# Where statistics, held results and late loads stand in the order of a routed expert kernel

## The chip, the cores and the metric

The kernel runs on one core of one Trainium2 chip. The metric is the device time of one execution in microseconds. The kernel before has a median of 445.12 us over three runs (444.80 to 446.07). One further execution was taken by the hardware profiler; its own time is 444.96 us, and its span, from the first instruction of the program to the last, is 443.2 us. All times inside the kernel are counted from the start of that span.

## The reference

The input x has 32 sequences of 256 tokens with 128 features: 8192 tokens. Two residual branches are computed, each behind a layer norm that is scaled and shifted per sequence.

```python
mod = (_silu(c) @ wmod).reshape(32, 6, 1, -1)
sa, ca, ga, sb, cb, gb = (mod[:, i] for i in range(6))
ga = (2 * (ga >= 0) - 1) * jnp.maximum(jnp.abs(ga), 0.25)      # gb likewise
h = _layernorm(x) * (1 + ca) + sa
g = sigmoid(h @ Wg.T + bg);  a = sigmoid(h @ Wd.T + bd);  v = h @ Wv.T + bv
x = x + ga * (prefix_scan((1 - a) * v, a) * g)                  # h_t = a_t h_{t-1} + x_t
h = _layernorm(x) * (1 + cb) + sb
logits = h @ gate_w.T + gate_b
vals, idx = top_k(softmax(logits), 2)                           # 2 of 8 experts
y[n, e] = relu(h[n] @ w1[e] + b1[e]) @ w2[e] + b2[e]            # hidden width 512
x = x + gb * sum over the two chosen experts of vals * y
```

The reference computes all eight experts for every token and gives six of them weight zero. The kernel computes the two chosen ones only, by sorting tokens to experts.

## The kernel before, in words

The 8192 tokens are cut into 16 supertiles of 512 tokens (s = 0 to 15). Each supertile passes through four steps, which the text calls by their functions: `a_norm` (statistics and normalisation for the first branch), `a_mix` (the first branch, with the scan), `a_res` (the residual, and the second layer norm) and `a_route` (logits, the choice of two experts, and the place of each of the 1024 token-expert pairs). The steps are written in a staggered order: round t does `a_norm(t)`, `a_mix(t-1)`, `a_res(t-2)` and `a_route(t-3)`; the first rounds follow the string `HEAD`. The routing of supertile s is called Rs below. Its last result that others wait for is `pi` (line 471), the rows to which the pairs go; just before it TensorE counts pairs into `pq` (line 454).

GpSimd then writes the rows of the pairs into a table in DRAM, `reg`, eight indirect DMAs for each supertile (line 499, `reg<-rw,pi`). All pairs of one expert lie together in `reg`. So the second branch works in blocks of 256 rows of one expert (68 blocks always, three more if the routing needs them). Some supertiles end with a small table (`table`) that says which blocks are full by then: 5 blocks after R2, 9 after R3, 13 after R4, then 17, 21, 25, 29 after R8, 37 after R10, 45 after R12, and all after R15.

A block passes through `b_load` (SyncE reads the block's expert and row from the table, loads the rows `xr`, line 584, and the expert's first weights `ww`, line 590), `b_in` (TensorE turns the rows into `pbx`, line 597, ScalarE and VectorE split them into `xs`, lines 599 and 600), `b_up` (twelve matmuls `p`, lines 617 to 619, and the activations `hh`) and `b_down` (sixteen matmuls `pby`, line 635, and the scaled result `yt`, line 639). Two indirect DMAs on GpSimd write a block's results to `yd` in DRAM (line 499 again, `yd<-yt,xi`), one row for each pair. One call of `b_step`, step i, does `b_in` of block i, `b_up` of block i-1 and `b_down` of block i-2, and loads up to four blocks ahead (`LOOK`). Five buffers hold `ww`, so the weights of block n wait for `b_up` of block n-5.

All indirect DMAs stand in one order on GpSimd: the scatters to `reg` and those to `yd` are numbered 1 to 264 in that order below (128 and 136). `drip` puts scatters to `reg` into it, one to three after each step. `results_out` puts scatters to `yd` into it, and leaves the youngest results back while routing is still going on. How many blocks' results stay back is the second argument in line 751:

```python
results_out(K * T, NJ * min(min(i - 1, EASE) + max(i - HOLD0, 0), HOLD) if alive or sending else max(len(results) - NJ, 0))
```

With `EASE` 3, `HOLD0` 24 and `HOLD` 9 that is three blocks up to step 24, then one more with each step, up to nine. A load of `xr` waits for the scatters to `reg` that stand before it when it is written (line 586).

At the end come the sums. A supertile's sum reads its two `yd` halves (`c_load`, line 705, tile `yk`, two DMAs of 256 KB), adds them, scales and adds the residual (`c_add`, lines 714, 696 and 716, tile `ot`, on VectorE), and stores the rows (line 717). `ended` holds the supertiles whose last block is done: block 52 ends supertiles 0 to 9, block 58 ends 10 to 12, block 62 ends 13, block 66 ends 14, and 15 comes after all. Each step loads one sum; the sum that was loaded three steps before (`CLAG`) is added in the same step. A `yk` load waits for all scatters to `yd` that stand before it.

The steps of the supertiles are written with priorities (`AHEAD`), and a list scheduler makes each engine's order from them. Within an engine the order is fixed from then on. One manual order is in it: the statistics of `a_norm` (`stats`, line 307) stay behind `placed[-1]`, the last entry of a list that `a_route` fills with its `pi` for the first three supertiles (line 472).

Of the kernel before, what the change touches and what calls it, by code (L numbers as in the profile page):

```python
# [17 lines left out]
ORDER = mybir.DependencyInfo(mybir.DependencyClass.NoSync, mybir.DependencyReason.DATA)  # L18
# [8 lines left out]
T = 4  # L27
# [6 lines left out]

XE = 3
EARLY = 3
PW = 3

AHEAD = (0, 200, 300, 400)
# [1 line left out]
BACK = 2  # L41
SKIP = 8

FIRST = 6
THREE = 7

ALWAYS = 68
# [4 lines left out]

EASE = 3
HOLD0 = 24
HOLD = 9
XRB = 9
OTB = 6
YTB = 7 + HOLD
CLAG = 3
HALF = 15  # L60

LN1G = {**{s: 1 for s in range(12)}, 12: 2, 14: 2}
# [3 lines left out]
def adaln_moe(ctx: ExitStack, tc: tile.TileContext, x, Wg, bg, Wv, bv, Wd, bd,  # L66
              gate_w, gate_b, w1, b1, w2, b2, c, wmod, out):
    nc = tc.nc
    NB, S, D = x.shape
    E, _, H = w1.shape  # L70
# [12 lines left out]
    of = out.rearrange("b s d -> (b s) d")  # L83
# [9 lines left out]
    def tokens(dram, r, n):  # L93
        return dram[r:r + n].rearrange("(q p j) d -> p q (j d)", p=P, j=JB)

    def tiles(t):
        return t.rearrange("p (q j) d -> p q (j d)", j=JB)
# [9 lines left out]
    xa = cp.tile([P, NS, T, D], F32, name="xa")  # L107
# [134 lines left out]
    def late_constants():  # L242
        b2f = wk.tile([P, T, D], F32, tag="ot", name="b2f", bufs=OTB)
        nc.gpsimd.memset(b2f, 0.0)
        for h in range(4):
            for j in range(T):
                r = (h * T + j) * E
                nc.sync.dma_start(b2f[r:r + E, j], b2)
        nc.vector.tensor_copy(b2x, b2f)
        lower = slice(P // 2, P)  # L250
        nc.vector.tensor_tensor(b2x[lower], b2f[lower], b2x[lower], op=ALU.subtract)


        sT3 = cp.tile([P, 3, NB], F32, name="sT3")
        nc.vector.tensor_copy(sT3, sT.unsqueeze(1).to_broadcast([P, 3, NB]))
        pr = psa.tile([P, 512], F32, tag="pz", bufs=2, name="pr")
        nc.tensor.matmul(pr[:N3, :D], sT3.rearrange("p a b -> p (a b)"), wm[:, 5 * D:], start=True, stop=True)
        mr = cp.tile([N3, D], F32, name="mr")
        guarded(mr, pr[:N3, :D], [N3, D], 1.0, "gr")
        nc.vector.tensor_copy(mr3, mr)  # L260
        for i in (1, 2, 2):
            w = slice(i * NB, (i + 1) * NB)
            nc.vector.tensor_tensor(mr[w], mr[w], mr3[w], op=ALU.subtract)
            nc.vector.tensor_copy(mr3[w], mr[w])

        nc.vector.tensor_tensor(sel, ident[:N3, 0:NB], ident[:N3, NB:2 * NB], op=ALU.add)
        nc.vector.tensor_tensor(sel, sel, ident[:N3, 2 * NB:N3], op=ALU.add)
# [29 lines left out]
    f = nc.sync.dma_start(reg[E * CAP:E * CAP + BLK].rearrange("(p t) d -> p t d", p=P), pad)  # L297
# [5 lines left out]
    def stats(mv, src, name, behind=None):  # L303
        n = src.shape[1]
        st = wk.tile([P, T, 6], F32, tag=f"st{name[0]}", name=f"st{name}")
        for j in range(n):
            w = nc.vector.bn_stats(st[:, j], src[:, j])
            if behind:
                tc.add_manual_dep(w.ins, behind.name, ORDER, reason="not ahead of the first supertiles that route")
        for j in range(n):  # L310
            nc.vector.bn_aggr(mv[:, j], st[:, j])

    def rsqrt(mv, name, s):
# [3 lines left out]
        def t1(nm, dt=F32):  # L317
            return wk.tile([P, n, 1], dt, tag=f"{nm}{name[0]}{n}", name=f"{nm}{name}")

        v, y, r = t1("nv"), t1("ny"), t1("nr")  # L320
        if s < PW:
            nc.vector.tensor_scalar(v, mv[:, :, 1:2], 1e-5, RSQ ** -2, op0=ALU.add, op1=ALU.mult)
# [17 lines left out]
    placed = []  # L340
    ln1 = {}

    def a_norm(s):
        g = LN1G.get(s, 0)
        if g:
            mv = wk.tile([P, g * T, 2], F32, tag=f"mva{g}", name=f"mva{s}")
            for i in range(g):
                stats(mv[:, i * T:(i + 1) * T], xa[:, s + i], f"a{s + i}", placed[-1] if placed else None)
            y, r = rsqrt(mv, f"a{s}", s)
            for i in range(g):  # L350
                ln1[s + i] = (y[:, i * T:(i + 1) * T], r[:, i * T:(i + 1) * T])
        y, r = ln1[s]
        xn = wk.tile([P, T, D], F32, tag="xn", name=f"xn{s}")
        for j in range(T):
            nc.scalar.activation(xn[:, j], xa[:, s, j], AF.Identity, scale=y[:, j], bias=r[:, j])  # L355
        return dict(s=s, xn=xn)

    def early(s, tag, name, bufs=1):

        if s < EARLY:  # L360
            return psb.tile([P, ST], F32, tag=tag, name=name, bufs=bufs)
# [54 lines left out]
    def a_route(a, base):  # L416
        s, xn = a["s"], a["xn"]
# [51 lines left out]
        nc.vector.tensor_reduce(pf, op_, axis=AX.X, op=ALU.add)  # L469
        pi = wk.tile([P, T * K], I32, tag="pi", name=f"pi{s}", bufs=3)  # L470
        w = nc.vector.tensor_copy(pi, pf.rearrange("p t k -> p (t k)"))
        if s < EARLY:
            placed.append(w.ins)
        sm = wk.tile([P, T], F32, tag="sm", name=f"sm{s}")
        nc.vector.tensor_reduce(sm, e8, axis=AX.X, op=ALU.add)
        rc = wk.tile([P, T], F32, tag="rc", name=f"rc{s}")
# [174 lines left out]
    results = []  # L651

    def results_out(most, left=0):

        for _ in range(min(most, len(results) - left)):
            results.pop(0)()

    def c_base(s):
# [21 lines left out]
        nc.tensor.matmul(pz, dgT, b2x.rearrange("p t d -> p (t d)"), start=True, stop=True)  # L680
        t = wk.tile([P, T, D], F32, tag="ot", name=f"tb2{s}", bufs=OTB)
        nc.scalar.activation(t.rearrange("p t d -> p (t d)"), pz, AF.Copy)
# [15 lines left out]
    def c_load(s):  # L698
        yk = wk.tile([P, T, K, RW], F32, tag="rw", name=f"yk{s}", bufs=4)
        yk = yk.rearrange("p t k r -> p (t k r)")[:, :K * T * D].rearrange("p (k t d) -> p k t d", k=K, t=T)  # L700
        step = JB if s >= HALF else T
        for j0 in range(0, T, step):
            for k in range(K):
                r = k * N + s * ST + j0 * P
                w = nc.sync.dma_start(tiles(yk[:, k, j0:j0 + step]), tokens(yd, r, step * P))
                tc.add_to_no_dep_group("yrows", w.ins)
        return s, yk, step

    def c_add(s, yk, step, queue):
        g = spread(s, "pz", 2)  # L710
        ot = wk.tile([P, T, D], F32, tag="ot", name=f"ot{s}", bufs=OTB)
        for j0 in range(0, T, step):
            js = slice(j0, j0 + step)
            nc.vector.tensor_tensor(ot[:, js], yk[:, 0, js], yk[:, 1, js], op=ALU.add)  # L714
            scaled(ot, g, range(j0 // JB, (j0 + step) // JB))
            nc.vector.tensor_tensor(ot[:, js], ot[:, js], xa[:, s, js], op=ALU.add)
            queue.dma_start(tokens(of, s * ST + j0 * P, step * P), tiles(ot[:, js]))


    blocks = []  # L720
    flow = []
    ended = []
    adding = []
    nload = 0
    based = 0
    sums = True
    LOOK = 4

    def b_step():

        nonlocal nload
        nonlocal based
        i = len(flow)
        while nload < len(blocks) and nload < i + 1 + LOOK:
            tb, q, ends = blocks[nload]
            blocks[nload] = b_load(nload, tb, q)
            blocks[nload]["ends"] = ends
            nload += 1
        b = blocks[i] if i < len(blocks) else None
        flow.append(b)  # L740
        if b:
            b_in(b)
        if i >= 1 and flow[i - 1]:
            b_up(flow[i - 1])
            drip(1 if alive else 3)
            if len(results) > NJ and not (alive or sending):
                results_out(1)
        if i >= 2 and flow[i - 2]:
            b_down(flow[i - 2])
            ended.extend(flow[i - 2]["ends"])  # L750
            results_out(K * T, NJ * min(min(i - 1, EASE) + max(i - HOLD0, 0), HOLD) if alive or sending else max(len(results) - NJ, 0))
        if not sums:
            return
        if not (alive or sending) and based < NS:
            c_base(based)
            based += 1
        if len(adding) >= CLAG or (adding and not ended and i >= len(blocks)):
            c_add(*adding.pop(0), nc.sync if i <= len(blocks) else nc.scalar)
        if ended:
            results_out(len(results))  # L760
            adding.append(c_load(ended.pop(0)))

    slot = 0
    alive = True
# [26 lines left out]
    for t, todo in enumerate(steps):  # L791
        def step3(s):
            nonlocal base, done
            with tc.high_priority(AHEAD[3] * (s >= EARLY)):
                base = a_route(st[s], base)
# [22 lines left out]
        def step2(s):  # L818
            with tc.high_priority(AHEAD[2] * (s >= EARLY)):
                a_res(st[s])  # L820

        def step1(s):
            with tc.high_priority(AHEAD[1] * (s >= EARLY)):
                a_mix(st[s])

        def step0(s):
            with tc.high_priority(AHEAD[0] * (s >= EARLY)):
                st[s] = a_norm(s)

        for i, s in todo:  # L830
            (step0, step1, step2, step3)[i](s)
            drip(3 if t < THREE else 2 if len(sending) > K * T else 1)
            if t >= FIRST:
                between()
# [59 lines left out]
```

## Time and profile before

| what | value |
|---|---|
| median of three runs | 445.12 us |
| profiled execution: its time / its span | 444.96 / 443.2 us |
| TensorE busy, matmuls (PE) | 366.6 us, 83% |
| TensorE busy, weight loads (PEld) | 321.5 us, 73% |
| VectorE (DVE) busy | 326.2 us, 74% |
| ScalarE (ACT) busy | 291.5 us, 66% |
| GpSimd (POOL) busy | 285.0 us, 64% |
| scatters to `reg`, `yd` (line 499) | 128 and 136, 986 and 1013 ns each |
| DMA over the span | 89.59 MB, 202 GB/s on average |

The page gives the busy share of each engine in 40 slices, the granted TensorE clock and the DMA rate in the same slices. The list of pieces in order of time gives, for each instruction, its start, its duration, the engine, the line, the tiles, and in brackets how long the engine sat idle before it and what ended that. A GpSimd scatter counts as busy for about 0.97 us, and the next one starts some 0.3 us after it.

### The profile page before, as it was taken

Reading aid. Unit: us, or ns where it says so; the run is one execution under the profiler, and the core shown is the slowest. Engines: PE = TensorE matmul, PEld = TensorE weight load, DVE = VectorE, ACT = ScalarE, POOL = GpSimd, SP = SyncE. Lnnn points to the kernel's source line nnn. Section 1 sums busy time; section 2 is a strip of 40 time slices with the busy share of each in tenths; the row PEclk is TensorE's granted clock in tenths of the full one; section 3 lists DMA queues with packets and bytes.
Section 4 is the critical chain, followed back from the end, with each engine's and each line's share of the span. In section 5 each row is a group of like instructions: output and inputs, shape, how many; then the busy total and the mean of one; then the engine's idle time right before and its main releaser. Section 6 shows DMA issues by size and latency. Waiting matters only on the chain.

```text
span 443.2 us, 11140 instructions
## 1 busy us (share of the span) xinstructions
PE 366.6 (83%) x2713; PEld 321.5 (73%) x2713; DVE 326.2 (74%) x1752; ACT 291.5 (66%) x721; POOL 285.0 (64%) x300
## 2 busy tenths in 40 slices
PE   4766465469999999999999999999389997499950
PEld 3333241328899889889989999999279997499940
DVE  6778889998878989978878877977337630346675
ACT  3765363476988998989778777666236666177630
POOL 4644857070577777777777777777777777555560
PEclk9988566588999999999999999999879999699995
DMA  7998311048438475655553886686189774799996
GB/s 196 370 321 248 137 42 45 4 123 297 150 96 246 124 209 169 182 161 173 172 173 114 260 277 197 185 275 173 50 265 304 219 221 148 233 342 362 352 271 197
DMA packets 54357, 89.59 MB, mean 202 GB/s; under 512 B 8366, under 2 KB 39292, under 8 KB 54294
## 3 DMA queue, kind: packets, MB, share of 16 engines
q1 hardware_dynamic: 44656, 70.87, 53.4%
q0 software_dynamic: 8480, 16.93, 10.8%
q10 hardware_dynamic: 1158, 1.07, 0.7%
q8 instruction: 25, 0.41, 0.4%
q14 instruction: 38, 0.31, 0.2%
HBM read 62.32 MB, written 27.04 MB: 202 GB/s over the span
## 4 chain that ended last, share of the span: by engine, by line
PE 57%; DMA 14%; DVE 11%; issue 6%; ACT 4%; POOL 4%; SPq 3%; POOLq 0%; DVEq 0%; ACTq 0%
PE pby L635 21%; PE pz L377 6%; PE p L617 6%; PE p L618 6%; PE p L619 6%; DMA yk<-yd 4%; DMA yd<-yt,xi 4%; PE pbx L597 3%; PE pl L428 3%; POOL reg L499 2%; DMA reg<-rw,pi 2%; PE pb L431 2%; DMA wr<-in_L_ffn_w_dram 2%; ACT xm L413 1%; POOL yd L499 1%
## 5 line engine op out<-in xcount | busy, mean ns | idle before, releaser
L499 POOL DMA_INDIRECT yd<-yt,xi x136 | 137.8, 1013 | 66.5 <-ACT yt L639 30.0
L499 POOL DMA_INDIRECT reg<-rw,pi x128 | 126.2, 986 | 61.6 <-issue 41.9
L635 PE MATMUL pby<-wr,hh 128*128 x1088 | 150.5, 276 | 0.3 <-ACT hh L625 0.3
L635 PEld LDWEIGHTS pby<-wr,hh 128*128 128x128 f32 x1088 | 137.7, 192 | 9.3 <-issue 6.9
L625 ACT ACTIVATE hh<-p,ww 128x256 f32<-128x256 f32 x219 | 93.1, 474 | 28.6 <-PE p L619 21.8
L617 PE MATMUL p<-xs,ww 128*128 128x256 f32 x272 | 86.2, 317 | 1.2 <-DVE cnt L798 0.3
L618 PE MATMUL p<-xs,ww 128*128 128x256 f32 x272 | 78.2, 288 | 0.0
L619 PE MATMUL p<-xs,ww 128*128 128x256 f32 x272 | 77.9, 287 | 0.0
L377 PE MATMUL pz<-h,wT 128*128 128x512 f32 x96 | 58.6, 728 | 3.7 <-ACT h L372 2.2
L639 ACT ACTIVATE yt<-pby,xr 128x128 f32<-128x128 f32 x136 | 42.7, 367 | 24.3 <-PE pby L635 24.3
L617 PEld LDWEIGHTS p<-xs,ww 128*128 128x128 f32 x272 | 52.5, 193 | 3.5 <-ACT ta L381 1.1
L618 PEld LDWEIGHTS p<-xs,ww 128*128 128x128 f32 x272 | 53.0, 195 | 0.5 <-issue 0.5
L619 PEld LDWEIGHTS p<-xs,ww 128*128 128x128 f32 x272 | 52.6, 193 | 0.2 <-issue 0.2
L597 PE MATMUL pbx<-ident,xr 128*128 128x128 f32 x136 | 27.1, 282 | 21.2 <-DMA xr<-reg 11.9
L600 DVE TENSOR_TENSOR xs<-pbx,xs 128x256 fp32r<-128x256 f32 x68 | 28.3, 416 | 20.4 <-ACT xs L599 20.2
L599 ACT ACTIVATE xs<-pbx 128x256 fp32r<-128x256 f32 x68 | 26.4, 388 | 20.2 <-PE pbx L597 20.1
L413 ACT ACTIVATE xm<-xa,nrb,nyb 128x128 f32<-128x128 f32 x64 | 26.5, 484 | 12.8 <-DVE nrb L336 12.8
L714 DVE TENSOR_TENSOR ot<-yk 128x512 f32<-128x512 f32 (+1 forms) x17 | 11.2, 658 | 31.4 <-DMA yk<-yd 30.8
L597 PEld LDWEIGHTS pbx<-ident,xr 128*128 128x128 f32 x136 | 17.1, 146 | 23.5 <-issue 9.9
L377 PEld LDWEIGHTS pz<-h,wT 128*128 128x128 f32 x96 | 19.4, 232 | 19.7 <-issue 12.9
L355 ACT ACTIVATE xn<-xa,nra,nya 128x128 f32<-128x128 f32 x64 | 26.4, 488 | 6.5 <-DVE nra L336 6.5
L623 DVE TENSOR_SCALAR hh<-p,ww 128x256 f32<-128x256 f32 x53 | 25.2, 476 | 5.0 <-ACT hh L625 4.7
(195 smaller groups left out, 645.8 us busy)
## 6 DMA issues: line engine op xcount, KB each, us to landing
ww<-wd SPq DMA_DIRECT2D x68, 514.0 KB
xr<-reg SPq DMA_DIRECT2D x68, 130.0 KB
yk<-yd SPq DMA_DIRECT2D x30, 256.0 KB
wd<-wh SPq DMA_DIRECT2D x8, 514.0 KB
xa<-in_L_attn_x_dram SPq DMA_DIRECT2D x16, 256.0 KB
out_dram<-ot SPq DMA_DIRECT2D x12, 256.0 KB
yd<-yt,xi POOLq DMA_INDIRECT x136
w1s<-in_L_ffn_w_dram SPq DMA_DIRECT2D x8, 256.0 KB
```

Of the source, the lines that this page charges most:

```text
L355: nc.scalar.activation(xn[:, j], xa[:, s, j], AF.Identity, scale=y[:, j], bias=r[:, j])
L377: nc.tensor.matmul(z, wT[:, i], h1, start=True, stop=True)
L413: nc.scalar.activation(xn[:, j], xt[:, j], AF.Identity, scale=y[:, j], bias=r[:, j])
L499: w = nc.gpsimd.indirect_dma_start(in_offset=None, **args).ins
L597: nc.tensor.transpose(px[:, j * P:(j + 1) * P], xr[:, j, 0:D], ident)
L600: w = nc.vector.tensor_tensor(xs[:, 1], px, xs[:, 0], op=ALU.subtract)
L617: nc.tensor.matmul(z, hi, xs[:, 0], start=True, stop=False)
L618: nc.tensor.matmul(z, hi, xs[:, 1], start=False, stop=False)
L619: nc.tensor.matmul(z, lo, xs[:, 0], start=False, stop=True)
L625: nc.scalar.activation(hh[:, k], p1[:, k - k0], AF.Relu, bias=bias)
L635: nc.tensor.matmul(py[:, j * D:(j + 1) * D], hh[:, k, j * P:(j + 1) * P], we[:, k * D:(k + 1) * D], start=(j == 0 and k == 0), stop=(j == ...
L639: nc.scalar.activation(yt[:, j], py[:, j * D:(j + 1) * D], AF.Copy, scale=xr[:, j, D:D + 1])
```

## The change

Four things change together.

- Statistics: `placed` gets the `pi` of every supertile, and the statistics of `a_norm(s)` stay behind the one of supertile s-5, though never behind one older than the third.
- Blocks: `FIRST` goes from 6 to 5, so that steps of blocks are written from round 5 on.
- Held results: `HOLD` goes from 9 to 14. `YTB`, the number of `yt` buffers, follows from 16 to 21; `OTB`, the number of `ot` buffers, goes from 6 to 5.
- Sums: the first step in which a supertile has ended puts all results into the order and only notes its number (`first`); loads begin `DELAY` = 3 steps later. While more than `MANY` = 5 supertiles are waiting, a step loads (and adds) two sums instead of one.

```diff
-FIRST = 6
+FIRST = 5
...
-HOLD = 9
+HOLD = 14
 XRB = 9
-OTB = 6
+OTB = 5
 YTB = 7 + HOLD
 CLAG = 3
+DELAY = 3
+MANY = 5
...
-                stats(mv[:, i * T:(i + 1) * T], xa[:, s + i], f"a{s + i}", placed[-1] if placed else None)
+                stats(mv[:, i * T:(i + 1) * T], xa[:, s + i], f"a{s + i}", placed[min(len(placed) - 1, max(s - BEHIND, EARLY - 1))] if placed else None)
...
-        if s < EARLY:
-            placed.append(w.ins)
+        placed.append(w.ins)
...
-        if len(adding) >= CLAG or (adding and not ended and i >= len(blocks)):
-            c_add(*adding.pop(0), nc.sync if i <= len(blocks) else nc.scalar)
-        if ended:
+        if ended and first is None:
             results_out(len(results))
-            adding.append(c_load(ended.pop(0)))
+            first = i
+        for _ in range(2 if len(ended) > MANY else 1):
+            if len(adding) >= CLAG or (adding and not ended and i >= len(blocks)):
+                c_add(*adding.pop(0), nc.sync if i <= len(blocks) else nc.scalar)
+            if ended and i >= first + DELAY:
+                results_out(len(results))
+                adding.append(c_load(ended.pop(0)))
```

`BEHIND` is 5. No instruction is added or removed: the same 264 scatters, 136 block loads, sums and matmuls run in another order.

More of the change, by code (lines that the diff above doesn't have):

```diff
@@ L36 @@
 EARLY = 3
+BEHIND = 5
 PW = 3
@@ L308, in stats @@
             if behind:
-                tc.add_manual_dep(w.ins, behind.name, ORDER, reason="not ahead of the first supertiles that route")
+                tc.add_manual_dep(w.ins, behind.name, ORDER, reason="not ahead of earlier supertiles that route")
         for j in range(n):
@@ L725, in adaln_moe @@
     based = 0
+    first = None
     sums = True
@@ L731, in b_step @@
         nonlocal nload
-        nonlocal based
+        nonlocal based, first
         i = len(flow)
```

## The prediction

> **What bounds the kernel now.** I read the slices first, then GpSimd's pieces in order of time, then the waits of SyncE's queue, then the two places where TensorE stands still.
>
> ```profile
> PE   4766465469999999999999999999389997499950
> POOL 4644857070577777777777777777777777555560
> PEclk9988566588999999999999999999879999699995
> 117.35 0.96 POOL L499 DMA_INDIRECT reg<-rw,pi  x1 [3.29 <-DVE stb L307]
> 318.64 0.96 POOL L499 DMA_INDIRECT reg<-rw,pi  x1 [0.30 <-DMA yd<-yt,xi]
> 383.63 1.45 POOL L499 DMA_INDIRECT yd<-yt,xi  x1 [0.30 <-issue]
> 388.63 1.12 POOL L499 DMA_INDIRECT yd<-yt,xi  x1 [3.54 <-ACT yt L639]
> ```
>
> TensorE is full from about 100 us. GpSimd's 7 looks loose, but it is full too: from 117.35 to 383.63 us a scatter follows every 1.30 us without a gap (35th to 240th: 266.3 us over 205). The 318.64 row is the last scatter to `reg`.
>
> ```profile
> SPq L584 <- DMA reg<-rw,pi: 106.6, 31, 18.3
> SPq L705 <- DMA yd<-yt,xi: 13.2, 6, 10.9
> 323.31 0.66 PE L597 MATMUL pbx<-ident,xr 128*128 128x128 f32 x2 [9.47 <-DMA xr<-reg]
> 378.20 0.92 SPq L705 DMA_DIRECT2D yk<-yd  x2
> 381.75 0.69 DVE L714 TENSOR_TENSOR ot<-yk 128x512 f32<-128x512 f32 x1 [13.20 <-DMA yk<-yd]
> 382.36 0.42 DVE L600 TENSOR_TENSOR xs<-pbx,xs 128x256 fp32r<-128x256 f32 x1
> 372.80:386.80 14.00, 5.10 (x35) 4.84 (x34) 2.96 (x9) 2.69 (x7) 9.54 (x10) 0.76 0.60 182
> 386.80:426.20 39.40, 38.96 (x345) 38.26 (x343) 24.91 (x59) 27.14 (x73) 21.71 (x21) 1.00 1.01 339
> ```
>
> Both standstills are GpSimd's lateness. Block 45 needs the last scatter to `reg` (318.64, landed 2.3 us later) and starts at 323.31, 9.5 us late. The first sum's load waits for the 234th scatter until 378.20; its add (381.75) stands before block 57's `xs` (382.36) on VectorE, so TensorE loses 8.9 us of the 14 from 372.8. From 386.8 the DMAs are full (share 1.01 at 339 GB/s; the last columns of the window rows are clock, share, rate). So GpSimd's place in its order, and then DMA bytes, set the end.
>
> **Part 1, statistics and earlier blocks.** In the built order, statistics of supertiles 8 to 11 leave the stretch between R2's `pi` and R3's logits: 16 of line 307 at 0.22 us, 16 of line 311 at 0.09, four rows of twelve small ones at 0.15, 9 to 12 us of VectorE work. Only supertile 8's four (0.9 us) stood before R3's last norm; the rest filled waits. In exchange block 0's rows come before R3's logits on TensorE: they need R2's last scatter (76.0 + 2.3), so `xr` issues at 78.5 and lands at 80.6; before, R3's logits began at 80.70. That cancels the 0.9 us. The moved work, 10 us, lands between 100 and 297 us, where VectorE is busy 166 of 197 us: nothing, while that slack lasts.
>
> The blocks are the real move. Blocks 0 to 5 now stand before R4's count. Between the counts of R3 and R4 the order has 78 up-matmuls at 0.13 us, 50 pairs of down-matmuls at 0.22, 6 line-377 pairs at 0.86, 38 transposes at 0.11, 4 logit pairs at 0.2: 31.5 us; before it was 17.5. (The same counting gives 162.1 us from R4 to R15 in the kernel before; the trace says 159.7.)
>
> ```profile
> 84.68 0.19 PE L454 MATMUL pq<-mk,tri 128*128 128x40 bf16 x1 [1.16 <-DVE mk L451]
> 114.08 0.18 PE L454 MATMUL pq<-mk,tri 128*128 128x40 bf16 x1
> 81.00:86.00 5.00, 3.77 (x21) 3.10 (x20) 4.75 (x48) 1.24 (x3) 0.00 (x0) 0.50 0.01 2
> 86.00:92.00 6.00, 3.86 (x8) 1.91 (x9) 6.00 (x57) 3.18 (x7) 2.39 (x3) 0.50 0.07 22
> 131.72 0.34 SPq L584 DMA_DIRECT2D xr<-reg  x1
> ```
>
> R3's count now follows twelve up-matmuls whose weights land at 83.5, so at 86.5 instead of 84.68. Here a rule is weighed. The rows say that TensorE stays at half clock until 92 us though it is busy 7.6 of 11 us; if it did so again, 5.5 us at half rate add 2.8: R4's count at 86.5 + 31.5 + 2.8 = 120.8. The Trainium skill, "TensorE: Matmul & The Clock Gate", section on the HAM clock gate, says that some 3.4 us of sustained work bring the full clock; work is now sustained from 81, so half rate ends near 86 and the count comes at 118.0. I take 119.5, between them, against 114.08. The first scatter of R4 (37th) follows 1.5 us later, as for R5 before (129.13, scatter at 131.14, less 0.5): 121.0 against 119.88. But both scatters of block 1 are done by then.
>
> **Part 2, waits that the new order makes.** Block 9's `pbx` now stands directly before R5's count. It needs R4's last scatter: from R4's count 1.5 us to the first, 8.9 to the eighth, 2.5 to the issue of `xr` (129.20 to 131.72), 2.1 to land: 15.0. TensorE has 12.4 us of work: it waits 2.6, and R5's first scatter is ready 16.7 us after R4's count, where GpSimd is free at 11.7. GpSimd loses 5.0 us; before, ten scatters stood between and it lost none. Block 13 waits for R6's first scatter likewise: 3.6 us of TensorE; block 17 for R7's: 3.5; block 29 for R10's rows: 4.9. GpSimd is behind by then and pays nothing for these at once.
>
> **Part 3, results kept back.** In the order no scatter to `yd` stands between the 123rd and the 156th: 34 to `reg` in a row, 10.4 us for each supertile. TensorE needs 61.0 us from R10's count to R14's, about 15 each. Before, 14 stood in a row and GpSimd had 20 us in hand at R10 (ready at 206.7, scattered at 226.4). After part 2 it has some 12. The stall at block 29 takes 4.9 of them, and TensorE from there to the counts of R12, R13, R14 has 5.9, 22.0 and 34.6 us: GpSimd waits 3.3, 5.8 and 2.4 us, 11.5 together. What is kept back would have filled this. If the cover were whole, this part would save: the last scatter to `reg` is the 178th instead of the 190th, 15.6 us earlier, and block 45 would not wait. With 1.1 + 5.0 + 11.5 lost it starts at 323.31 - 15.6 + 17.6 = 325: nothing gained.
>
> **Part 4, the sums.** `yk` loads now wait for the 240th scatter instead of the 234th, and stand after the loads of blocks 60 to 63. Time of the 240th: 383.63 + 1.1 + 5.0 + 11.5 = 401.2; landed 2.3 later: 403.5 against 378.20. VectorE's first two adds stand before block 61's `xs`. TensorE is through block 60 near 388 and then stands 22 us (before: 14, at block 57). Behind it are ACT's `hh`, the scatters of blocks 61 to 67, and the last sums. From 403.5: 16 sums of 0.524 MB in and 0.262 out, five weights of 0.526, four `xr`, some 24 scatters of 0.066: 17.3 MB; at 339 GB/s 51 us, plus 2 for the last add and store: 53. (Before, 19.6 MB from 378.20 by this sum: 60; it took 65.) TensorE's seven blocks with two adds in each (two times 2.2 us on VectorE) end near 403.5 + 38 and lie under it. Fewer `ot` buffers: a store is out some 5 us after its add, five buffers of 2.2 us each cover twice that; else up to 3 us. End of span 456.5; the profiled time was 1.8 above its span, and the median 0.2 above that: **458 us**.
>
> **Bounds of the unknown.** GpSimd's loss: not below 0; not above 30 (34 scatters at TensorE's pace of 15 for each supertile, plus 8 at R5). Nearest row: the 16.5 worked out. The tail: 50 if DMA runs at the best rate of the page (362 GB/s), 60 by the last stage before.
>
> **The rivals.** *Faster:* GpSimd loses nothing. For it speaks that TensorE starts blocks 14 us earlier and that GpSimd never starved before. Then the 240th scatter is at 384.7, the loads at 387, the end at 440: 442 us. It decides at one point: the 240th scatter before 386.5, thus less than 2 us lost after R4. Against it: the wait at block 9 needs only the order and four durations. *Half:* GpSimd loses 8: 449 us; R12 to R14 come early enough because a stall I counted is not there. *Worse:* the paired adds hold TensorE longer and loads, stores and weights share full DMAs: 8 to 10 us on top, 467. *The change does nothing:* only if both POOL losses and the head's gain are nil; the same 445, since the later loads (+9) eat the tail's saving (-12).
>
> **How the numbers follow.** Likeliest 0.65 (own range 450 to 465), half 0.15, faster 0.12, worse 0.05, nothing 0.03. Within 0.3% (1.3 us), about what a measurement tells from no change: 0.04 with the edge of half; slower 0.84. The range leaves out faster and most of worse: 444 to 467.
>
> **What would show it.** R4's count at 118 to 121. A GpSimd gap of 4 to 6 us before R5's first scatter, and gaps before R12 to R14. Block 45 near 325. The first `yk` issue near 403, one TensorE gap of about 20 us before block 61. Then DMA share about 1. Wrong if GpSimd has no gap after R4, or if the first `yk` comes before 388.

## The result, and the profile after

The changed kernel takes 467.5 us (median of four runs, 465.51 to 470.32), the kernel before 445.27 us beside it: a ratio of 1.049 (95% interval 1.044 to 1.054), slower by 22 us. The forecast was 458 us with a range up to 467. The direction was right; the median lies 9.5 us above the forecast and half a microsecond above the range, which is less than the runs differ among themselves. The profiled execution took 465.51 us with a span of 463.4 us. Line numbers of the changed kernel are three or four higher than before (GpSimd's scatters are now line 502).

The slices of the page, for TensorE, GpSimd and the granted clock:

```profile
PE   4756774999959959999998999957999999339960
POOL 3645854170326777777777445777777777774550
PEclk9877556699978979999999999976999999859995
```

Each slice is 11.6 us. Before, GpSimd read 7 without a break from the twelfth slice to the 34th. Now it has holes (3 and 2 in slices eleven and twelve, 4 and 4 in slices 23 and 24), TensorE has a 5 in slices 12, 15 and 27, and the clock dips with it.

GpSimd's pieces in order of time, the ones with more than 0.9 us of idle time before them between 110 and 410 us:

```profile
121.68 0.96 POOL L502 DMA_INDIRECT reg<-rw,pi  x1 [16.30 <-ACT hh L628]
140.26 0.96 POOL L502 DMA_INDIRECT reg<-rw,pi  x1 [8.51 <-issue]
262.88 0.95 POOL L502 DMA_INDIRECT reg<-rw,pi  x1 [4.37 <-ACT h L376]
281.39 0.96 POOL L502 DMA_INDIRECT reg<-rw,pi  x1 [8.17 <-ACT hh L628]
```

These are the first scatters of R4, R5, R12 and R13. With the usual 0.3 us taken off, GpSimd stands 8.2 us before R5, 4.1 before R12 and 7.9 before R13: 20.2 us together, where the kernel before lost 0.7 at these three places (at R5). R4's first scatter, the 37th, is 1.8 us later than the 37th was before (119.88).

TensorE in order of time, the counts of R3, R4, R5 and R13 and the places that the forecast spoke of:

```profile
87.27 0.26 PE L458 MATMUL pq<-mk,tri 128*128 128x40 bf16 x1
118.97 0.18 PE L458 MATMUL pq<-mk,tri 128*128 128x40 bf16 x1
135.38 0.69 PE L600 MATMUL pbx<-ident,xr 128*128 128x128 f32 x2 [3.85 <-DMA xr<-reg]
135.86 0.24 PE L458 MATMUL pq<-mk,tri 128*128 128x40 bf16 x1
254.62 0.44 PE L600 MATMUL pbx<-ident,xr 128*128 128x128 f32 x2 [1.88 <-DMA xr<-reg]
276.71 0.18 PE L458 MATMUL pq<-mk,tri 128*128 128x40 bf16 x1
337.62 0.38 PE L600 MATMUL pbx<-ident,xr 128*128 128x128 f32 x2
413.37 0.37 PE L693 MATMUL gtpz<-mr,sel 96*128 96x128 bf16 x2 [15.51 <-DVE ot L699]
```

R4's count is at 118.97 (forecast 119.5). Block 9 (135.38) waits for its rows right before R5's count, as the forecast said. Block 29 starts at 254.62 and R13's count follows 22.1 us later. Block 45 is the row at 337.62. The one long stand near the end is the last row; it comes behind block 61's `pbx` (394.94), not before it.

SyncE's first load of a sum, and then, from the table of stretches, the stretch from that load to the end (columns as before: length, busy time of PE, PEld, DVE, ACT, POOL, clock, DMA share, GB/s):

```profile
407.95 1.94 SPq L708 DMA_DIRECT2D yk<-yd  x4
```

```profile
408.00:463.00 55.00, 33.25 (x258) 30.21 (x257) 36.30 (x80) 19.16 (x52) 24.01 (x23) 0.81 0.91 307
```

The first load comes 29.8 us later than before (378.20), and from it to the end of the span pass 55.4 us instead of 65.0: 20.2 us later in all, the whole loss of the span.

### The profile page after: what moved, and what is told of

Same layout as the page of the kernel before. It is cut to its first block, busy times and chain, and to the rows that moved or that the text cites. A ratio compares the mean times of both kernels' runs of the same rounds, so it can differ in the third digit from the quotient of the medians.

```text
span 463.4 us, 11078 instructions
## 1 busy us (share of the span) xinstructions
PE 378.7 (82%) x2713; PEld 326.7 (71%) x2713; DVE 327.2 (71%) x1752; ACT 293.8 (63%) x721; POOL 285.4 (62%) x300
## 4 chain that ended last, share of the span: by engine, by line
PE 52%; DMA 13%; DVE 6%; issue 5%; POOL 5%; ACT 3%; SPq 1%; POOLq 0%; DVEq 0%; ACTq 0%
PE pby L638 20%; PE p L620 6%; PE p L621 6%; PE p L622 6%; DMA yd<-yt,xi 5%; PE pz L381 5%; DMA yk<-yd 3%; PE pbx L600 3%; POOL reg L502 2%; DMA reg<-rw,pi 2%; POOL yd L502 2%; DMA xr<-reg 2%; PE pl L432 2%; PE po L409 1%; PE pb L435 1%
## 5 line engine op out<-in xcount | busy, mean ns | idle before, releaser
L638 PE MATMUL pby<-wr,hh 128*128 x1088 | 153.0, 278 | 0.5 <-ACT hh L628 0.3
L600 PE MATMUL pbx<-ident,xr 128*128 128x128 f32 x136 | 28.7, 295 | 14.6 <-DMA xr<-reg 10.5
```

What stands on the lines that cost most here:

```text
L600: nc.tensor.transpose(px[:, j * P:(j + 1) * P], xr[:, j, 0:D], ident)
L638: nc.tensor.matmul(py[:, j * D:(j + 1) * D], hh[:, k, j * P:(j + 1) * P], we[:, k * D:(k + 1) * D], start=(j == 0 and k == 0), stop=(j == ...
```

## The experiments

The theory when the runs began: TensorE does blocks that wait for rows in front of the counts that GpSimd waits for; GpSimd, in its fixed order, has then nothing to send, and what it loses moves the 240th scatter, the first load of a sum and the end. The rivals: the later, paired sums cost the time; the fourteen results kept back cost it by themselves; the earlier blocks cost it by themselves. Ratios are to the kernel before, run on the same chip in the same session, with 95% intervals.

### Undoing one part: nine results kept back

```diff
-HOLD = 14
+HOLD = 9
```

> The changed kernel with nine blocks' results kept back instead of fourteen; everything else as changed. In the built order the run of scatters to the routed rows without a result between them is then 18 (from the 123rd) instead of 33. Theory A (GpSimd's fixed order runs dry: part of the loss is the wait for R12 and R13, 4.4 and 8.2 us of idle time in the changed kernel's trace): both gaps shrink to under 2 us, the 240th scatter and the first load of a sum come about 12 us earlier (near 396 against 407.95), the end with them: 455 us (451 to 459). Theory B (the sums' later and paired loads cost the time, not GpSimd's gaps): the gaps may go, but the time stays at 464 to 468. Theory C (only the earlier blocks cost, by the wait at block 9): 464 to 468 as well, with the gaps at R12 and R13 still there because TensorE is late.

Measured: 461.46 us, ratio 1.035 (1.028 to 1.042). The gap before R12 stayed (5.18 us at 263.57), the one before R13 fell from 8.17 to 3.04. The first load came at 403.24, 4.7 us earlier instead of 12. So some 6 us of the loss hang on the number kept back; 16 remain, and the time lies between the ranges of theory A and of its rivals. Theory A had both gaps under 2 us: R13's shrank, though not so far, and R12's did not, so that one does not depend on what is kept back.

### Undoing one part: blocks from the sixth round

```diff
-FIRST = 5
+FIRST = 6
```

> The changed kernel with blocks from the sixth round as before; all else as changed. Theory A with the whole loss begun at block 9: R5's first scatter follows without a gap (8.5 us in the changed kernel), TensorE does not stand at blocks 9 and 13 and its clock stays full there, so that R12 and R13 come in time too; the first load of a sum near 390, the time 447 us (443 to 452). Theory C' (fourteen results kept back starve GpSimd by themselves, wherever TensorE stands): the gaps before R12 and R13 stay or grow to 15 us or more, the time 457 to 462. Theory B (sums): 460 to 466.

Measured: 447.73 us, ratio 1.0047 (1.0018 to 1.0077). Nearly all of the loss is gone. GpSimd's gaps in that version:

```profile
126.48 0.96 POOL L502 DMA_INDIRECT reg<-rw,pi  x1 [4.78 <-ACT h L376]
261.97 0.96 POOL L502 DMA_INDIRECT reg<-rw,pi  x1 [5.32 <-ACT hh L628]
```

R4's first scatter is at 109.22, R5's gap is 4.78, R12 has none, and R13's first scatter is 19.4 us earlier than in the changed kernel; the first load (387.69) is 20.3 us earlier. On TensorE only the `pbx` of blocks 0 to 3 now stand before R4's count (in the changed kernel those of blocks 0 to 8), and block 29 stands behind R12's count instead of before it. So without the earlier blocks the other three parts cost next to nothing. Theory A had the time right, but expected no gap at R5, where 4.78 us stay, and R13 in time, where 5.3 us stay with fourteen kept back.

### Undoing one part: the sums

The step is put back as it was:

```diff
-        if ended and first is None:
-            results_out(len(results))
-            first = i
-        for _ in range(2 if len(ended) > MANY else 1):
...
+        if len(adding) >= CLAG or (adding and not ended and i >= len(blocks)):
+            c_add(*adding.pop(0), nc.sync if i <= len(blocks) else nc.scalar)
+        if ended:
+            results_out(len(results))
+            adding.append(c_load(ended.pop(0)))
```

> The changed kernel with the sums' loads and adds as before (one sum each step from the first block past, no delay, no pairs); all else as changed. Theory A: GpSimd's order and its gaps are those of the changed kernel; the first load waits for the 234th scatter instead of the 240th, so it comes 8 us earlier (near 400), and the tail from it is about 63 instead of 55.5: 465 us (461 to 469), no gain. Theory B (the delay and the pairs cost the time): 447 to 455.

Measured: 465.14 us, ratio 1.0428 (1.0375 to 1.0481), whose interval overlaps that of the changed kernel. First load at 402.25, tail 62.8, as theory A had it. Theory B is out: the sums are not the cause.

### One part alone: blocks from the fifth round

```diff
-FIRST = 6
+FIRST = 5
```

on the kernel before.

> The kernel before with one edit: blocks from the fifth round. The order of GpSimd's scatters is that of the changed kernel up to the 140th. Theory A: TensorE stands at block 9 for R4's rows, GpSimd is idle 4 to 9 us before R5's first scatter, and the sums' first load (234th scatter) comes that much later than before (378.20): 383 to 388; tail 65 as before: 452 us (449 to 457). Rival (the wait at block 9 is caught up later, GpSimd having slack): 443 to 447, with a first load near 378. Rival (the loss needs the statistics' new order too, since they stand between R5's positions and its gates): gap under 2 us here, 444 to 447.

Measured: 457.95 us, ratio 1.030 (1.024 to 1.037): slower by itself, more than expected, but not in the place expected.

```profile
127.19 0.96 POOL L499 DMA_INDIRECT reg<-rw,pi  x1 [13.75 <-ACT xs L599]
139.04 0.95 POOL L499 DMA_INDIRECT reg<-rw,pi  x1 [1.53 <-issue]
277.68 0.96 POOL L499 DMA_INDIRECT reg<-rw,pi  x1 [4.21 <-ACT hh L625]
254.14 0.66 PE L597 MATMUL pbx<-ident,xr 128*128 128x128 f32 x2 [7.08 <-DMA xr<-reg]
```

In this order blocks 0 to 3 stand even before R3's count (94.63, before 84.68), so R4's first scatter is at 127.19 (its place in the order was at 119.88 before) and R5's gap only 1.53. GpSimd loses at R4 instead of R5. Then TensorE stands 7.08 us at block 29 (last row), which is in front of R12's count here too, and R13 comes late again. The first load is at 389.94, where theory A had 383 to 388. The statistics' new order is not needed for the loss; it only moves where the first part of it falls.

### Taking away the wait at block 9

```diff
-        if slot % SKIP and len(blocks) - len(flow) > BACK:
+        if slot % SKIP and slot != 9 and len(blocks) - len(flow) > BACK:
```

> The changed kernel with the ninth place for a block left empty, so that in the built order R5's count stands before block 9's first transpose instead of behind it; blocks 0 to 8 still stand before R4's count. Theory A1 (the wait at block 9 for R4's rows, and TensorE's half clock after it, make the loss at R5): the gap before R5's first scatter falls from 8.5 us to 2 to 4, TensorE does not stand 3.85 us at block 9, the supertiles from R6 on and the first load of a sum come 5 to 8 us earlier (400 to 403), 461 us (457 to 463). Theory A2 (R4's own lateness behind nine blocks is the loss; the wait only moves to the next block): the gap at R5 shrinks, but R6 or R7 has one of 3 us or more in its place, 464 to 468.

Measured: 463.38 us, ratio 1.038 (1.031 to 1.045).

```profile
136.77 0.96 POOL L502 DMA_INDIRECT reg<-rw,pi  x1 [2.79 <-issue]
262.75 0.96 POOL L502 DMA_INDIRECT reg<-rw,pi  x1 [6.66 <-ACT h L376]
281.11 0.96 POOL L502 DMA_INDIRECT reg<-rw,pi  x1 [8.14 <-ACT hh L628]
252.50 0.55 PE L600 MATMUL pbx<-ident,xr 128*128 128x128 f32 x2 [4.87 <-DMA xr<-reg]
```

The gap at R5 fell from 8.51 to 2.79, as theory A1 said. But R4's eight scatters now stand two places earlier in GpSimd's order, for nearly the same first time (121.30), which takes back 2.2 us: R10's first scatter is only 2.3 us earlier (233.32 against 235.59). And R12's gap grew by 2.3. R13's first scatter is at 281.11 as against 281.39, and the first load is 1.1 us earlier, not 5 to 8. So taking the wait away is worth next to nothing at the end: A1's time was wrong, and A2's new gap at R6 or R7 did not come either. (The scheduler also moved block 28's `pbx` behind R11's count, so the edit is not quite the wait alone.) Where its gain went is seen at block 29: TensorE stood there 4.87 us (last row) instead of 1.88, and this is what its clock did (columns: length, PE busy, clock, DMA share, GB/s):

```profile
252.00:254.00 2.00, 1.50 (x8) 0.66 0.82 298
254.00:256.00 2.00, 2.00 (x12) 0.50 0.98 269
256.00:258.00 2.00, 2.00 (x11) 0.50 0.90 307
260.00:262.00 2.00, 2.00 (x24) 1.00 0.97 312
```

TensorE was ready for R10's rows 5.1 us earlier than in the changed kernel (at 247.6) and got them 2.1 us earlier, but then worked at half clock until about 259: from block 29 to R12's count it took 8.1 us instead of 6.2, so that the count came at 260.63 against 260.85.

### Statistics behind the gates

```diff
-        w = nc.vector.tensor_copy(pi, pf.rearrange("p t k -> p (t k)"))
-        placed.append(w.ins)
+        nc.vector.tensor_copy(pi, pf.rearrange("p t k -> p (t k)"))
...
-        nc.vector.tensor_copy(rw[:, :, :, D], gates)
+        w = nc.vector.tensor_copy(rw[:, :, :, D], gates)
+        placed.append(w.ins)
```

> The changed kernel with the moved statistics tied to the copy of the gates into the rows instead of to the positions, so that VectorE does not do them between a supertile's positions and its gates. In the changed kernel R5's positions are cast at 136.98 and its gates copied at 139.32, so the first scatter is at 140.26. Theory A3 (that queue on VectorE is 2 us of R5's loss and as much before R13): the gaps before R5 and R13 shrink by 1.5 to 2.5 us each, 463 us (461 to 466). Rival (the statistics then come late for the norms that need them, or something else on VectorE stands there): unchanged, 465 to 469.

Measured: 471.62 us, ratio 1.058 (1.051 to 1.064); not faster. At R5 the queue did shrink by the 2 us of theory A3: the first scatter (139.97) follows the count (137.52) by 2.45 us instead of 4.40. But the count itself came 17.6 us after R4's instead of 16.9, so the gap is 7.60 instead of 8.51. R13's scatter follows its count by 4.7 us as before, its gap is 8.16: its queue is not made of the moved statistics. And TensorE stood 5.68 us at block 29 and took 8.4 us from there to R12's count, so R12's gap grew to 7.09. A3 is right for the queue at R5 and wrong for R13 and for the time. The edit is not that queue alone: in TensorE's order it also moved block 8's `pbx` behind R4's count and block 28's behind R11's.

### The other parts alone, first in a disturbed session

Four edits on the kernel before, in one session: the statistics' order alone, the sums alone, fourteen kept back alone (with `OTB` 5), and statistics and sums together.

> The kernel before with one edit: the statistics' new order behind earlier supertiles. Theory A (the earlier blocks are the loss; the statistics' order by itself is a gain): R4's first scatter at 106 to 109 us as with blocks from the sixth round in the changed kernel (106.15), against 117.35 before; some 4.5 of the 11 us are given back before R5, up to 3 before R13; the first load of a sum (234th scatter) near 374, tail 65 as before: 442 us (438 to 445). Rival (the head's gain is wholly lost again at R5 and R13, since TensorE sets when supertiles route): 444 to 447 with a first load near 378. Rival (the moved statistics stand in VectorE's way later): 448 or more.

> The kernel before with one edit: the sums start three steps later and go in pairs when more than five wait. Theory A: GpSimd's series is that of before; the first load waits for the 240th scatter (383.63) and comes near 386, the tail from it lasts 55 us as in the changed kernel: 443 us (441 to 446). Theory B (delay and pairs cost the time): the tail stays at 62 to 65, 450 to 454.

> The kernel before with one edit: fourteen blocks' results kept back instead of nine (and five buffers for the sums' results instead of six, to make room). The last scatter to the routed rows is then the 180th instead of the 190th. Theory A: GpSimd is late enough in the kernel before (20 us in hand at R10) to find R12 and R13 ready, so no gap over 3 us; block 45 starts near 312 instead of 323.31 and TensorE does not stand there, but the sums still wait for the 234th scatter at the same time: first load near 378, 445 us (443 to 448). Theory C' (fourteen kept back starve GpSimd by themselves): gaps of 8 to 12 us before R12 and R13, 453 to 457. Rival (block 45's wait was part of what sets the end): 438 to 441.

> The kernel before with the statistics' new order and the later, paired sums, but blocks from the sixth round and nine results kept back. Theory A: the gap of 5.3 us before R13 that the version with blocks from the sixth round had goes, since 16 scatters to the routed rows stand in a row instead of 29; first load of a sum near 383, tail 55.5: 440 us (437 to 444), under the kernel before. Rival (R13's gap has TensorE's lateness as its cause and stays): 445 to 448.

In that session every kernel took a third longer, the one before included (590.03 us), so none of the times expected there can be compared. The ratios were 1.047 (1.039 to 1.055), 0.999 (0.995 to 1.003), 1.000 (0.996 to 1.004) and 1.050 (1.045 to 1.056). The profiles show TensorE idle for up to 9.4 us with nothing that it waits for, here with the sums alone, where VectorE and ScalarE were idle from 186 to 194 us too, while GpSimd went on:

```profile
195.00 0.80 PE L637 MATMUL pby<-wr,hh 128*128 x2 [9.44 <-issue]
```

Why is open. The four edits ran again in later sessions, where the kernel before took 445 us; the conclusions rest on those.

### The other parts alone, again

The statistics' order alone:

```diff
+BEHIND = 5
...
-                stats(..., placed[-1] if placed else None)
+                stats(..., placed[min(len(placed) - 1, max(s - BEHIND, EARLY - 1))] if placed else None)
...
-        if s < EARLY:
-            placed.append(w.ins)
+        placed.append(w.ins)
```

> The statistics' order alone once more, since the other three of its group ran while every kernel took a third longer. Theory A as told there: R4's first scatter at 106 to 109 us, first load of a sum near 374, 442 us (438 to 445). Rival (the gain of the head is lost again before R5 and R13): 444 to 447. Rival (the order loses by itself, as it did there by 4.7%): 455 to 467.

Measured: 444.75 us, ratio 0.997 (0.994 to 1.000). R4's count came at 107.90 instead of 114.08, its first scatter at 109.75 instead of 117.35. Then R5 had a gap of 4.78 us (0.98 before), and the first load came at 376.46, only 1.7 us earlier than before, with a tail 1.6 longer. The first rival holds, that the gain of the head is lost again; 3.5 of its 7.6 us went before R5, where GpSimd now came first and waited for R5's rows.

The sums alone (the lines of the change that touch `b_step`, on the kernel before):

> The later, paired sums as the only edit on the kernel before, once more. Theory A: 240th scatter as before (383.63), first load near 386, 8 us later than before, tail 55 to 57 instead of 65: 443 us (441 to 445). Theory B (delay and pairs cost time): the tail stays over 60, 448 or more.

Measured: 442.08 us, ratio 0.992 (0.989 to 0.996). First load at 383.77, tail 55.9. A gain, as theory A had it: 5.6 us of waiting against 9.1 of tail.

Fourteen results kept back alone:

```diff
-HOLD = 9
+HOLD = 14
...
-OTB = 6
+OTB = 5
```

> Fourteen results kept back as the only edit on the kernel before, once more. Theory A (the gaps before R12 and R13 come from block 29's rows standing ahead of R12's count, which only the new orders do; here block 29 comes after R12's count and R4 routes at 117): no gap over 3 us, block 45 near 312 to 315 instead of 323.31, first load near 378, 445 us (443 to 448). Theory C' (fourteen kept back starve GpSimd by themselves): gaps of 5 us or more before R13, 450 to 457. Rival (block 45's wait was part of what sets the end): 438 to 441.

Measured: 444.87 us, ratio 0.9995 (0.9965 to 1.0026). TensorE in order of time:

```profile
312.05 0.38 PE L597 MATMUL pbx<-ident,xr 128*128 128x128 f32 x2
380.88 0.69 PE L597 MATMUL pbx<-ident,xr 128*128 128x128 f32 x2 [20.31 <-DVE xs L600]
```

The first row is block 45. It starts 11.3 us earlier than before and does not wait; GpSimd has no gap at R12 or R13. And nothing is gained: TensorE comes to block 58 that much sooner and stands there 20.31 us in one piece, instead of 9.47 at block 45 and 8.90 at block 58 before. Here block 29 stands behind R12's count. So keeping fourteen back does not starve GpSimd by itself, and the wait at block 45 was never part of what sets the end.

Statistics and sums together, and the same with eleven kept back (`HOLD` 11, `OTB` 5):

> Statistics' order and sums together, blocks from the sixth round, nine results kept back, once more for the same reason. Theory A: first load of a sum near 383, tail 55.5, 440 us (437 to 444). Rival (R13's gap stays): 445 to 448. Rival (the order loses by itself): 455 to 467.

> Statistics' order and sums with eleven results kept back instead of nine (five buffers for the sums' results); 21 scatters to the routed rows stand in a row instead of 16. Theory A: the last of them is the 186th instead of the 190th, so block 45's wait shrinks from 4.2 to 0 to 1 us, but the first load waits for GpSimd's 240th scatter as with nine, and R13 may add a gap of up to 2 us: first load 382 to 385, 442 us (440 to 445), no gain over the 441.6 with nine. Rival (block 45's wait counts): 436 to 439.

Measured: 441.58 us, ratio 0.989 (0.983 to 0.996), and 445.88 us, ratio 1.001 (0.997 to 1.005). With nine, no gap of over 1 us is left between R5's and the tail, and the first load is at 382.53. With eleven, R13's gap is back (2.73 us at 261.94) and the first load is at 385.32; block 45 still waits 4.30 us, where 0 to 1 were expected. The version with nine is 1.1% under the kernel before; its interval overlaps that of the sums alone, so no gain of the statistics' order on top of them is shown. With eleven the gain is gone.

## Why the forecast was right in kind and short in size

The step that failed is one term, the lag of 1.5 us from a supertile's count on TensorE to its first scatter. It measured 2.7 us at R4, 4.4 at R5 and 4.7 at R13. Of R5's 4.4, 2.0 come from the moved statistics, which Part 1 had put at nothing. So GpSimd lost 8.2 us at R5 instead of 5.0: that is 3.2 of the 4.5 us by which the first load came later than forecast; the tail was put 2.4 too short.

The four traces in which fourteen results are kept back beside the new sums agree on what sets the end:

| version | R13's first scatter | first load | from scatter to load | from load to end |
|---|---|---|---|---|
| changed kernel | 281.39 | 407.95 | 126.6 | 55.4 |
| one slot skipped | 281.11 | 406.82 | 125.7 | 55.2 |
| statistics behind the gates | 285.94 | 412.22 | 126.3 | 57.9 |
| blocks from the sixth round | 261.97 | 387.69 | 125.7 | 55.7 |

From R13 on GpSimd runs without a gap to the 240th scatter. What was lost before counts only through the time at which R13 can be sent. In the changed kernel R10's rows reach block 29 at 254.62, TensorE works 22.1 us from there to R13's count, and the first scatter goes out 4.7 us after that.

**Part 1, the head: right.** R4's count was forecast at 119.5 and came at 118.97, between the two values that the rule on the clock and the rows gave (118.0 and 120.8). Neither fitted the clock itself: it rose near 89 us (0.77 on average from 88 to 90, 0.50 before), where the rule had 86 and the rows 92. The first scatter was 0.7 us later than forecast, since it followed the count by 2.7 us instead of 1.5.

**Part 2, the wait at block 9: right in place, too small.** Forecast were 2.6 us of standing on TensorE and 5.0 lost on GpSimd; the trace has 3.85 and 8.2. R5's count came 16.9 us after R4's instead of 15.2; 1.2 of these 1.7 us are R4's lag (2.7 instead of 1.5), which moves R4's last scatter and with it block 9's rows. R5's own lag of 4.4 us adds 2.9 more. GpSimd was free 13.1 us after R4's count instead of 11.7, so the loss grew by 1.7 + 2.9 - 1.4 = 3.2. The row that the 1.5 was read from had 2.0 in it:

```profile
129.13 0.18 PE L454 MATMUL pq<-mk,tri 128*128 128x40 bf16 x1
131.14 0.96 POOL L499 DMA_INDIRECT reg<-rw,pi  x1 [0.98 <-ACT yt L639]
```

GpSimd had sat idle 0.98 us in front of that scatter of R5, so the half microsecond that the forecast took off was part of the lag. VectorE in the changed kernel, in order of time:

```profile
136.98 0.17 DVE L475 CAST pi<-pf 128x8 int32<-128x8 f32 x1
137.42 0.67 DVE L311 BATCH_NORM_STATS2 sta<-xa 128x6 f32<-128x128 f32 x3
139.32 0.17 DVE L482 COPY rw<-idg 128x8 f32<-128x8 f32 x1
```

The positions are cast 1.1 us after the count. They are not the last thing that others wait for: a scatter also needs the gates in its rows, and these come 2.3 us later, behind a supertile's statistics, a block's `xs` and the block table. "Nothing, while that slack lasts" was said of VectorE's average over 197 us; at this place it had no slack. With the statistics tied behind the gates, 2 of these microseconds went.

What the forecast left out, though it did not make this loss, is that a stand can be followed by half clock (columns as above):

```profile
132.00:134.00 2.00, 0.00 (x0) 0.82 0.10 33
136.00:138.00 2.00, 1.16 (x11) 0.50 0.90 278
140.00:142.00 2.00, 2.00 (x4) 0.50 0.88 278
144.00:146.00 2.00, 2.00 (x15) 1.00 0.24 74
```

The Trainium skill, "TensorE: Matmul & The Clock Gate", in its part on the HAM clock gate, says that one idle window of about 3.4 us brings TensorE back to half rate; here the clock fell about 1.8 us after TensorE stopped (131.5 to 133.3, by the first row). The forecast used that section for the warm-up at the head and not for the stands that it forecast itself. Up to the stand the clock was full (1.00 from 118 to 132), and block 9 waited for rows, so R5's count owes the half clock a few tenths at most. The work behind was slowed. TensorE therefore stood less at the later blocks: 1.88 us at block 29 where 4.9 were forecast, and not at block 17 where 3.5 were. But at block 29 it still waited for R10's rows, and GpSimd had sent without a gap from R5 to those, so the half clock after blocks 9 and 13 did not move the changed kernel's end. It counted where the stand at block 29 itself was long, with one slot skipped and with the statistics behind the gates: there it stood between block 29 and the counts of R12 and R13.

**Part 3, the results kept back: right in mechanism, sizes mixed.** From block 29 to the counts of R12, R13 and R14 the forecast had 5.9, 22.0 and 34.6 us; the trace has 6.2, 22.1 and 34.6. The gaps were forecast at 3.3, 5.8 and 2.4, 11.5 together; they were 4.1, 7.9 and none, 12.0. That the sums agree is luck: R13 came out 2.1 too small and R14 2.4 too large. With R4's 1.8 and R5's 8.2 that is 22.0 of lateness where the forecast had 17.6. R13 failed by the same lag, 4.7 us instead of 1.5, and this could have been read before. In the trace of the kernel before, R13's count is at 252.49, and VectorE shows

```profile
254.88 0.15 DVE L471 CAST pi<-pf 128x8 int32<-128x8 f32 x1
256.42 0.14 DVE L479 COPY rw<-idg 128x8 f32<-128x8 f32 x1
```

so its gates came 3.9 us after its count, behind the residual and the second layer norm's statistics of the next supertile. GpSimd had its backlog then and nobody waited. The 1.5 was taken from R5 alone. In the changed kernel the same pieces stand there, and the positions come last:

```profile
280.46 0.16 DVE L475 CAST pi<-pf 128x8 int32<-128x8 f32 x1
```

The runs also put the shares right. The forecast added R5's loss and the gaps before R12 to R14 as terms. They add up in the trace, but they do not come off one by one: removing R5's alone gave 1.1 us at the first load. The earlier blocks cost 3.0% alone, the number kept back nothing alone (0.9995), statistics and sums together gain 1.1%; the sum of these is 1.9%, the change costs 4.9%. The rest, 3.0%, exists only together. Some 1.4 of it go with nine kept back (3.5%); the other 1.6 belong to the earlier blocks with statistics and sums, and no run splits these. What the traces show of it: the earlier blocks put block 29, which waits for R10's rows, ahead of R12's count, and late rows then make R12 and R13 late; the fourteen kept back take away what GpSimd could have sent meanwhile.

**Block 45: wrong, without effect.** Forecast 325, measured 337.62. SyncE's queue has the eight fills of `reg` (line 576, from 300.62) ahead of block 39's load, and those need R15's final counts (299.71); block 39's rows were issued at 312.17. Before, the same fills stood there, but TensorE had blocks 35 to 38 to do meanwhile and block 39 (290.11) did not wait. TensorE worked less than 13 of the 20 us from 302 to 322. The forecast did not put these fills into that step. The end did not wait for it but for GpSimd; TensorE only stood less near the end, 15.51 us instead of the forecast 22.

**Part 4, the tail: short by 2.4.** 55.4 us against 53, with a DMA share of 0.91 instead of about 1. The forecast's own sum gave 60 for the kernel before, where 65.0 were measured, so that it came out short could be seen. The gain of the later sums was real (442.08 us with the sums alone).

The terms together: the first load 4.5 us later than forecast, the tail 2.4 longer, the profiled execution 2.1 above its span instead of 1.8, and the median 2.0 above the profiled execution instead of 0.2, where the kernel before had been taken as the measure; half a microsecond was rounded away. That is 9.5.

Three small readings were off without effect: 33 scatters to `reg` stand in a row from the 123rd, not 34; in the kernel before it was 12, not 14; and GpSimd's series before had one gap, the 0.98 us at R5.

Of the rivals, *faster* decided at less than 2 us of loss after R4 and *half* had 8 us of loss; both were far off. *Worse* named nearly the time measured, 467, but for a cause that did not happen: it had the tail 8 to 10 us longer, and that was 2.4.

## What to carry to other kernels

When an engine with a fixed order runs dry, look for the one piece of work whose readiness it waits for last (here R13's rows); removing an earlier gap is worth only what arrives there. A lag such as "from the count to the first scatter" is to be read at each place where it will count, also where it is hidden now, since it shows as soon as the backlog in front of it is gone. And a stand of TensorE can cost more than its length: reckon the half clock behind it too, where something waits for TensorE next (8.1 and 8.4 us instead of 6.2 from block 29 to R12's count).

## What the runs showed of the hardware that was not expected

- Many stands of TensorE were followed by a granted clock of 0.50, but their length alone did not decide. Those of 3.15 us (block 13 of the changed kernel, with 2.46 more three microseconds later), 3.85, 4.87, 5.68 and 7.08 us were; one of 1.88 us (block 29 of the changed kernel) was not. But one of 2.43 us (block 0 of the kernel before) was not either, and one of 2.23 us (block 17 with one slot skipped) was, with the columns as above:

```profile
182.00:184.00 2.00, 0.22 (x3) 1.00 0.71 157
184.00:186.00 2.00, 2.00 (x13) 0.59 0.89 304
```

- The clock fell about 1.8 us after TensorE stopped at block 9 of the changed kernel, and 5.0 us after it stopped at block 29 with one slot skipped. After work began again it took about 2.9 us until the clock was full at block 58 of the kernel before, and 8.2 and 7.0 us at those two; the last two are longer than the 3.4 us of sustained work that the page of the Trainium skill named above gives. Estimated from the busy time in those stretches of the changed kernel (7.8 us from 134 to 144 and 5.2 from 166 to 174, nearly all at half rate), the stands at blocks 9 and 13 cost TensorE some 6 us on top of their 7.
- In the session in which every version took a third longer, a scatter to `reg` was as long as ever (978 ns with the sums alone, 987 for the same kernel later), much of the time went into stands without a visible cause, and the statistics' order, harmless elsewhere, cost 4.7% there.
